# A two-layer graph network on one core: tiles of a half chunk multiplied in reverse, added in forward order, and PSUM banks split by layer

## The chip, the cores and the metric

The kernel runs on one core of one Trainium2 chip. The metric is the device time of one execution in microseconds (us); the time of a kernel is the median of several runs. Beside them there is one profiled execution, taken by the hardware profiler, with its own time and its trace. Engines are called PE (TensorE: matmuls; its weight loads are PEld), DVE (VectorE), ACT (ScalarE), POOL (GpSimd) and SP (SyncE).

## The reference

Two layers of a relational graph convolution over 50,000 nodes with 128 features each, 850,000 edges and 16 relations, then a residual and a layer norm. The weight matrix of each relation is a mix of 8 basis matrices.

```python
def _rgcn_layer(h, src, dst, rel, basis, w_comp, loop_w, bias):
    W = jnp.einsum('rb,bio->rio', w_comp, basis)
    seg = dst * N_REL + rel
    agg = jax.ops.segment_sum(h[src], seg, num_segments=N_ENT * N_REL)
    agg = agg.reshape(N_ENT, N_REL, -1)
    msg = jnp.einsum('nri,rio->no', agg, W)
    return relu(msg + h @ loop_w + bias)

h = _rgcn_layer(x, src, dst, rel, basis1, w_comp1, loop_w1, bias1)
h = _rgcn_layer(h, src, dst, rel, basis2, w_comp2, loop_w2, bias2)
x = _layernorm(x + h, axis=-1, eps=1e-5)
```

The edges come sorted by dst. 50,000 of them are self loops, one for each node, which the kernel handles without a gather; the other 800,000 are gathered, 800,000 / 128 = 6,250 tiles a layer.

## The kernel before

**Tiling.** The features are kept transposed: 128 features on the partitions. A tile is 128 edges in a row (sorted by dst, so that they end in at most WN = 12 neighbouring nodes). Ten tiles (K) are a chunk, five (PER) a half chunk; there are 625 chunks (C) in a layer and 12,500 tiles in all. The layer loop is at L917, the loop over chunks at L1000 and below.

**What is done for a tile.**

- *Gather* (L254, called at L1006). POOL issues an indirect DMA that fetches the 128 source rows. It does so for chunk c+2 while chunk c is multiplied, and a chunk's ten tiles go into one of four buffers g (GATHERS), so tile i lies where tile i-40 lay. Each DMA reports on one of eight semaphores in turn, called lanes below.
- *hot_of* (L923, L930). DVE builds, for a whole chunk, a 128 x 960 matrix `hot`: for each edge its eight basis weights, placed in the column of its node.
- *Multiply* (L1018). PE multiplies g by hot (128x128 by 128x96, float32; the trace shows two weight loads and two matmuls for it) into a piece of a PSUM bank. Five tiles share a bank.
- *Add* (L950). DVE adds the 128 x 96 product to `ring`, an SBUF array with sums for 3 x 512 nodes, at a place read from a register; the registers are loaded at L944, for 20 tiles at a time. An add isn't issued at once: it is put in the list `behind` with a due time of BEHIND = 12 tiles later, and `added_up_to` issues what is due.

**The work of a group** of 512 nodes (98 a layer, about one in 64 tiles) is planned in `Group.planned` with due times counted in tiles: in layer 1 `load`, `turn` (PE transposes, L726) and `combine` (L743); in both `widen` (a broadcast of 1 MB by DMA), `lay` (ACT copies the node features into a bank, L770), `own` (DVE writes the self-loop part into ring from it, L775), `copy` (ACT takes the finished sums out of ring, L792), eight `base` matmuls (L798), `loop` (L803), `relu` (L810), `back` (PE transposes, L822) and `store` (L830 in layer 1). `Weights` makes the per-edge weights for four chunks: in layer 1 `multiply` (L668) and `keep` (L682), in layer 2 a load of what layer 1 stored.

**The order.** PE, POOL, DVE and ACT run their instructions in the order in which the program issues them; what is inserted between are the waits on semaphores. One instruction can carry some of its waits; what is more becomes a wait instruction of its own ahead of it on that engine.

**Banks.** Six PSUM banks named `pa` are handed out by `Turns`: a new one at each half chunk (L1016), and for turn, combine, lay, back and multiply, all from one row in the order of the calls. When `take` hands out a bank again, it first issues the work that must still read it: for a half chunk `Once(added_up_to, ...)`, the adds up to the half's last tile. Six takes later a bank comes round again, which is six halves or fewer, as other work took banks in between.

Of the kernel before, what the change touches and what calls it, by code (L numbers as in the profile page):

```python
# [40 lines left out]
F32 = mybir.dt.float32  # L41
# [7 lines left out]
PSUM = bass.MemoryType.PSUM  # L49
DRAM = bass.MemoryType.DRAM  # L50

P = 128
# [3 lines left out]
K = P // WN  # L56
# [9 lines left out]
PER = 5  # L66
Q = AT // 2
BANK = 512
# [8 lines left out]
BEHIND = 12  # L77
AFTER = 18
AT_ONCE = 4
WIDE = 1  # L80
PARTS_OF = ((0, 3), (3, 5))
# [8 lines left out]
def tile_rgcn_resnorm(  # L90
# [129 lines left out]

    ps_a = ctx.enter_context(tc.tile_pool(name="ps_a", bufs=6, space=PSUM))
    ps_f = ctx.enter_context(tc.tile_pool(name="ps_f", bufs=1, space=PSUM))
# [6 lines left out]
    class Turns:  # L229
        def __init__(self, pool, name, count):  # L230
            self.pool, self.name, self.count, self.held = pool, name, count, []

        def take(self, read=None):

            if len(self.held) == self.count:
                first = self.held.pop(0)
                if first is not None:
                    first()
            self.held.append(read)
            return self.pool.tile([P, BANK], F32, name=self.name)  # L240

# [8 lines left out]

    banks = Turns(ps_a, "pa", 6)

# [5 lines left out]
    def turned(h, m, sb):  # L258

        tp = ps_a.tile([P, BANK], F32, name="pa")  # L260
        nc.tensor.transpose(tp[:, :m], h, ident[:m, :m])
        hT = sb.tile([P, P], F32, name="hT")
        nc.scalar.copy(hT[:, :m], tp[:, :m])
        return hT[:, :m]
# [342 lines left out]
    def chunked():  # L607
        with (
# [20 lines left out]
            class Weights:  # L629
# [32 lines left out]
                def multiply(self):  # L662
                    m = self.m
                    self.po = [banks.take(self.keep) for _ in PARTS_OF]
                    for po, (j0, j1) in zip(self.po, PARTS_OF):
                        of = po[:, : 2 * AT * (j1 - j0) * NB].rearrange("e (n t w) -> e n t w", n=2, t=AT)
                        for j in range(j0, j1):
                            nc.tensor.matmul(  # L668
                                of[:, :, :, (j - j0) * NB : (j - j0 + 1) * NB],
                                self.is_rel[:m, j * P : (j + 1) * P],  # L670
                                each[:m],
                                start=True,
                                stop=True,
                            )
# [17 lines left out]
            class Group:  # L692
# [29 lines left out]
                def turn(self):  # L722
                    m = self.m
                    self.po = banks.take(self.keep)
                    for j in range(J):
                        nc.tensor.transpose(self.po[:, j * P : j * P + m], self.h[:m, j, :], ident[:m, :m])  # L726
# [14 lines left out]
                def combine(self):  # L741
                    self.comb = banks.take(self.combined)
# [25 lines left out]
                def lay(self, b):  # L768
                    self.laid[b] = banks.take(self.owns[b])
                    nc.scalar.copy(self.laid[b][:, : self.cnt], self.hT[:, : self.cnt])  # L770
# [46 lines left out]
                def back(self):  # L817
                    m = self.m
                    self.po = banks.take(self.kept)
                    by_place = self.oT[:, : self.cnt].rearrange("o (p j) -> o j p", j=J)  # L820
# [96 lines left out]
            for n, of in enumerate((x, H1)):  # L917

                def hot_of(c):
# [16 lines left out]
                    hots[c] = hot  # L936

                def add(c, k, pa):

                    i = c * K + k  # L940
                    if i % (2 * K) == 0:
                        left = min(2, C - c) * K
# [54 lines left out]
                for c in range(C):  # L997
# [15 lines left out]
                    hot = hots.pop(c)  # L1013
                    for k in range(K):
                        if k % PER == 0:
                            pa = banks.take(Once(added_up_to, c * K + k + PER - 1))  # L1016
                        if k < ks(c):
# [6 lines left out]
                            )  # L1024
                            behind.append((c * K + k + BEHIND, (c, k, pa)))
                        added_up_to(c * K + k - BEHIND)
                        if c or k == K - 1:
                            go_on(c * K + k)
                    if n == 0 and c == 3:
# [5 lines left out]
                while events or behind:  # L1035
                    added_up_to(now - BEHIND)
                    go_on(now)
                    now += 1
                banks.held = [None] * len(banks.held)
            ordered.close()  # L1040

    def summed():
        L1 = dram.tile([N, D], F32, name="L1")
        L2 = dram.tile([N, D], F32, name="L2")
        with tc.tile_pool(name="io", bufs=2) as io, tc.tile_pool(name="sbf", bufs=2) as sb:
# [73 lines left out]
            def added(h, n, L):  # L1119


                def block(r0, p):
# [13 lines left out]
                    for e in range(ROW):  # L1136
# [4 lines left out]
                        for b in range(NB):  # L1141
                            if b % (BANK // D) == 0:
                                mb = ps_a.tile([P, BANK], F32, name="pa")
                                nc.tensor.matmul(
# [13 lines left out]
                        at = tf[:p, e : e + 1]  # L1158
                        tp = ps_a.tile([P, BANK], F32, name="pa")
                        nc.tensor.transpose(tp[:p, :p], at.to_broadcast([p, p]), ident[:p, :p])  # L1160
# [82 lines left out]
```

## Time and profile before

| | us |
|---|---|
| median of 3 runs | 18,209.43 |
| lowest and highest | 18,202.78, 18,209.78 |
| the profiled execution | 18,065.77 |
| its span, first to last instruction | 18,063.9 |
| mean granted clock of PE | 0.602 of full speed |

In the profile, a group of instructions is a line of the kernel, an engine and an operation, "out<-in" by names, and then the count, the busy time and the mean duration of one in ns, and behind the second bar the idle time of the engine just before these instructions with the releaser that ended most of it. "issue" means that the engine waited for nothing that the profile shows; "remote" is a releaser that it can't name. The chain that ended last is followed back from the last instruction, with shares of the span. A gather moves 128 rows of 512 bytes; all DMA together moved 1,527 MB, 85 GB/s in the mean, and the 16 DMA engines were busy for about 30% of the span, 18.0% with the gathers' queue.

The first gather of layer 1 starts at 58 us, the last of layer 2 ends at 18,023 us. Layer 2 cannot gather before layer 1's last store to H has landed; its first gather starts at 9,110 us.

### The profile page before, as it was taken

The numbers are of one execution on the slowest core, as the hardware profiler recorded it, in microseconds if no ns is written. First come the engines' busy times: TensorE is split into PE (matmuls) and PEld (weight loads), VectorE is DVE, ScalarE is ACT, GpSimd is POOL, SyncE is SP. The second block draws the span as 40 slices with busy tenths as digits, with TensorE's granted clock in tenths as the row PEclk, the third lists the DMA queues.
The fourth block names the chain that finished last, engine by engine and source line by source line (L and its number), as shares of the span: only waits on it lengthen the run. The fifth ranks groups of instructions, "written<-read, shape, count | busy, mean of one in ns | idle before, by whom it ended". The sixth has DMA issues, their size and how long they took to land.

```text
span 18063.9 us, 132710 instructions
## 1 busy us (share of the span) xinstructions
PE 8315.7 (46%) x31484; PEld 6301.1 (35%) x31484; DVE 6563.7 (36%) x18253; ACT 1621.0 (9%) x2256; POOL 11861.6 (66%) x12540
## 2 busy tenths in 40 slices
PE   3444444444444444444444444444444444444444
PEld 2333333333333333333333333333333333333333
DVE  5444444443333333333333333333333333333333
ACT  0110011110100000010000000000000000000000
POOL 6666666666666666666666666666666666666665
PEclk7666666666666666666655555555555555555556
DMA  3333333333323322232322222222222222222222
GB/s 100 94 95 92 92 95 95 94 88 89 85 84 85 85 85 82 85 88 83 84 78 81 81 82 79 81 81 81 81 80 80 81 81 81 81 81 81 81 81 67
DMA packets 793018, 1527.32 MB, mean 85 GB/s; under 512 B 229924, under 2 KB 296342, under 8 KB 792230
## 3 DMA queue, kind: packets, MB, share of 16 engines
q0 software_dynamic: 403552, 826.82, 18.0%
q1 hardware_dynamic: 386934, 691.33, 11.6%
q8 instruction: 259, 4.24, 0.1%
q14 instruction: 529, 4.33, 0.1%
q10 hardware_dynamic: 1744, 0.60, 0.0%
HBM read 1390.97 MB, written 126.86 MB: 84 GB/s over the span
## 4 chain that ended last, share of the span: by engine, by line
issue 37%; PE 28%; another core or an unknown queue 16%; POOL 8%; DVE 5%; DMA 3%; ACT 1%; DVEq 1%; POOLq 0%; ACTq 0%; SPq 0%
PE pa L1018 18%; POOL g L254 8%; PE pn L798 8%; DVE ring L950 2%; DMA g<-H,src 2%; DVE ring L775 1%; PE pa L668 1%; PE pn L803 1%; DMA g<-in_x_dram,src 1%; ACT own L792 0%; PE pa L822 0%; DVE fixed L330 0%; DVEq L944 0%; DVE word L333 0%
## 5 line engine op out<-in xcount | busy, mean ns | idle before, releaser
L1018 PE MATMUL pa<-hot,g 128*128 128x96 f32 x25000 | 5704.8, 361 | 7613.1 <-issue 5607.3
L1018 PEld LDWEIGHTS pa<-hot,g 128*128 128x128 f32 x25000 | 5201.3, 276 | 9323.7 <-issue 7321.4
L254 POOL DMA_INDIRECT g<-in_x_dram,src x6250 | 5929.4, 949 | 3046.5 <-issue 1432.7
L254 POOL DMA_INDIRECT g<-H,src x6250 | 5895.2, 943 | 3045.9 <-issue 1428.8
L950 DVE TENSOR_TENSOR ring<-pa,ring 128x96 f32 x12500 | 3212.4, 257 | 10941.4 <-PE pa L1018 5215.2
L798 PE MATMUL pn<-own,basis 128*128 128x512 f32 x3104 | 2237.5, 799 | 508.1 <-issue 486.0
L930 DVE TENSOR_TENSOR hot<-pm,fixed 128x960 f32<-128x960 f32 x1250 | 1443.0, 1154 | 78.9 <-remote 19.2
L792 ACT COPY own<-ring 128x4096 f32<-128x4096 f32 x194 | 699.6, 3606 | 3172.0 <-DVE ring L950 2131.9
L775 DVE TENSOR_TENSOR ring<-wide,pa 128x2048 f32<-128x2048 f32 x392 | 893.7, 2280 | 84.1 <-issue 28.8
L798 PEld LDWEIGHTS pn<-own,basis 128*128 128x128 f32 x3104 | 656.1, 250 | 701.3 <-issue 696.3
L770 ACT COPY pa<-hT 128x512 f32<-128x512 f32 x392 | 230.8, 589 | 3035.4 <-DVE ring L950 1349.5
L726 PE MATMUL pa<-ident,rows 128*128 128x128 f32 x392 | 107.7, 420 | 829.6 <-ACT t L830 452.2
L810 ACT ACTIVATE oT<-pn,bias_of 128x512 f32<-128x512 f32 x196 | 134.3, 685 | 3928.0 <-PE pa L1018 2237.0
L668 PE MATMUL pa<-each,is_rel 128*128 128x128 f32 x1570 | 348.4, 377 | 291.8 <-issue 151.4
L668 PEld LDWEIGHTS pa<-each,is_rel 128*128 128x128 f32 x1570 | 300.5, 276 | 324.0 <-issue 226.2
L726 PEld LDWEIGHTS pa<-ident,rows 128*128 128x128 f32 x392 | 74.6, 223 | 845.1 <-ACT t L830 457.0
L923 DVE TENSOR_TENSOR fixed<-fixed,key 128x120 f32<-128x120 f32 x1250 | 350.4, 280 | 0.1
L822 PE MATMUL pa<-ident,oT 128*128 128x128 f32 (+1 forms) x784 | 218.6, 406 | 201.4 <-issue 133.9
L803 PE MATMUL pn<-hT,loop 128*128 128x512 f32 x392 | 263.1, 740 | 50.1 <-issue 49.9
L682 ACT COPY pm<-pa 128x192 f32<-128x192 f32 x628 | 141.0, 304 | 1063.8 <-remote 903.3
L822 PEld LDWEIGHTS pa<-ident,oT 128*128 128x128 f32 (+1 forms) x784 | 146.7, 219 | 230.2 <-issue 206.0
L597 ACT ACTIVATE sd<-mv,eps 128x4 f32<-128x4 f32 x98 | 29.1, 297 | 1929.9 <-DVE st L594 969.3
(129 smaller groups left out, 1655.8 us busy)
## 6 DMA issues: line engine op xcount, KB each, us to landing
wide<-CW SPq DMA_DIRECT2D x388, 1024.0 KB
g<-in_x_dram,src POOLq DMA_INDIRECT x6250
g<-H,src POOLq DMA_INDIRECT x6250
rows<-in_x_dram SPq DMA_DIRECT2D x194, 256.0 KB
PM<-pm SPq DMA_DIRECT2D x157, 160.0 KB
pm<-PM SPq DMA_DIRECT2D x157, 160.0 KB
H1T<-oT SPq DMA_DIRECT2D x97, 256.0 KB
H<-t SPq DMA_DIRECT2D x97, 256.0 KB
```

The source lines that it names most:

```text
L254: return nc.gpsimd.indirect_dma_start(out=to, out_offset=None, in_=of, in_offset=bass.IndirectOffsetOnAxis(ap=idx, axis=0))
L668: nc.tensor.matmul(of[:, :, :, (j - j0) * NB : (j - j0 + 1) * NB], self.is_rel[:m, j * P : (j + 1) * P], each[:m], start=True, stop=True,)
L770: nc.scalar.copy(self.laid[b][:, : self.cnt], self.hT[:, : self.cnt])
L775: nc.vector.tensor_tensor(ring[:, b : b + AT_ONCE, self.at : self.at + cnt], self.wide.pop(b)[:, :, :cnt], self.laid.pop(b)[:, None, :cnt] ...
L792: nc.scalar.copy(self.sums, ring[:, :, at : at + cnt])
L798: nc.tensor.matmul(self.pn[:, : self.cnt], BASIS[:, b, :], self.sums[:, b, :], start=b == 0, stop=False)
L803: nc.tensor.matmul(self.pn[:, : self.cnt], LOOP, self.hT[:, : self.cnt], start=False, stop=True)
L822: nc.tensor.transpose(self.po[:m, j * D : (j + 1) * D], by_place[:, j, :], ident)
L923: nc.vector.tensor_tensor(own[:, : ks(c)], grid[:, None, :].to_broadcast([P, ks(c), WN]), key[:, c * K : c * K + ks(c), None].to_broadcast ...
L930: nc.vector.tensor_tensor(hot[:, : ks(c)], pm[:, c % BATCH * K : c % BATCH * K + ks(c), :, None].to_broadcast([P, ks(c), NB, WN]), own[:, ...
L950: nc.vector.tensor_tensor(into, pa[:, k % PER * NB * WN : (k % PER + 1) * NB * WN].rearrange("d (b w) -> d b w", w=WN), into, op=OP.add,)
L1018: nc.tensor.matmul(pa[:, k % PER * NB * WN : (k % PER + 1) * NB * WN], g[:, k, :], hot[:, k].rearrange("e b w -> e (b w)"), start=True, st ...
```

## The change

The change has five parts that belong together.

- Each half chunk's tiles are multiplied last one first: k = 4, 3, 2, 1, 0 and 9, 8, 7, 6, 5. The last chunk of a layer keeps the old order.
- The adds of a half are issued in forward order, k = 0 to 4, the reverse of PE's: each new one is put in front of the half's others in `behind`, and all five carry the due time of the half's end plus BEHIND, where each tile had its own.
- The six banks are six fixed tiles with a counter for each set of banks that is asked for, in place of a pool that turns by itself. `SECTIONS` gives the tiles of layer 1 all six banks, those of layer 2 banks 0 to 3; `OTHERS` gives the other work of layer 1 all six, that of layer 2 (lay, back) banks 4 and 5. `multiply` and `combine` exist in layer 1 only and take its entry. In layer 1 all callers share one counter over six banks, as before.
- The registers with the places are loaded when an add of a new pair of chunks comes, whichever tile that is (`pair`), where it was the pair's first tile.
- At a layer's end the counters are cleared.

```diff
+SECTIONS = (
+    ((6, True, True),),
+    ((4, True, True),),
+)
+OTHERS = (None, (4, 5))
...
     class Turns:
-        def __init__(self, pool, name, count):
-            self.pool, self.name, self.count, self.held = pool, name, count, []
-
-        def take(self, read=None):
-
-            if len(self.held) == self.count:
-                first = self.held.pop(0)
-                if first is not None:
-                    first()
-            self.held.append(read)
-            return self.pool.tile([P, BANK], F32, name=self.name)
+        def __init__(self, tiles):
+            self.tiles, self.held, self.turn = tiles, [None] * len(tiles), {}
+
+        def take(self, read=None, among=None):
+
+            among = tuple(among or range(len(self.tiles)))
+            at = among[self.turn.get(among, 0) % len(among)]
+            self.turn[among] = self.turn.get(among, 0) + 1
+            if self.held[at] is not None:
+                self.held[at]()
+            self.held[at] = read
+            return self.tiles[at]
...
-    banks = Turns(ps_a, "pa", 6)
+    banks = Turns([ps_a.tile([P, BANK], F32, name=f"pa{i}") for i in range(6)])
...
-                    self.po = banks.take(self.keep)
+                    self.po = banks.take(self.keep, OTHERS[self.n])
...
-                    self.laid[b] = banks.take(self.owns[b])
+                    self.laid[b] = banks.take(self.owns[b], OTHERS[self.n])
...
-                    self.po = banks.take(self.kept)
+                    self.po = banks.take(self.kept, OTHERS[self.n])
...
+                pair = [None]
+
                 def add(c, k, pa):
 
                     i = c * K + k
-                    if i % (2 * K) == 0:
+                    if (n, i // (2 * K)) != pair[0]:
+                        pair[0] = n, i // (2 * K)
                         left = min(2, C - c) * K
                         offs = batches[c // BATCH].offs
                         nc.vector.load(at_reg[:left], offs[0:1, c % BATCH * K : c % BATCH * K + left])
...
-                    for k in range(K):
-                        if k % PER == 0:
-                            pa = banks.take(Once(added_up_to, c * K + k + PER - 1))
+                    for at in range(K):
+                        part = SECTIONS[n][c * len(SECTIONS[n]) // C]
+                        k = at // PER * PER + (PER - 1 - at % PER if part[1] and c + 1 < C else at % PER)
+                        if at % PER == 0:
+                            pa = banks.take(
+                                Once(added_up_to, c * K + at + PER - 1), range(part[0])
+                            )
                         if k < ks(c):
                             nc.tensor.matmul(
                                 pa[:, k % PER * NB * WN : (k % PER + 1) * NB * WN],
...
-                            behind.append((c * K + k + BEHIND, (c, k, pa)))
-                        added_up_to(c * K + k - BEHIND)
-                        if c or k == K - 1:
-                            go_on(c * K + k)
+                            if part[2] and c + 1 < C:
+                                behind.insert(len(behind) - at % PER, (c * K + at // PER * PER + PER - 1 + BEHIND, (c, k, pa)))
+                            else:
+                                behind.append((c * K + at + BEHIND, (c, k, pa)))
+                        added_up_to(c * K + at - BEHIND)
+                        if c or at == K - 1:
+                            go_on(c * K + at)
...
                 banks.held = [None] * len(banks.held)
+                banks.turn.clear()
```

More of the change, by code (lines that the diff above doesn't have):

```diff
@@ L219, in weighed @@
             nc.vector.tensor_copy(split[:, n], mine)
-    ps_a = ctx.enter_context(tc.tile_pool(name="ps_a", bufs=6, space=PSUM))
+    ps_a = ctx.enter_context(tc.tile_pool(name="ps_a", bufs=1, space=PSUM))
     ps_f = ctx.enter_context(tc.tile_pool(name="ps_f", bufs=1, space=PSUM))
@@ L258, in turned @@
     def turned(h, m, sb):
-        tp = ps_a.tile([P, BANK], F32, name="pa")
+        tp = banks.take()
         nc.tensor.transpose(tp[:, :m], h, ident[:m, :m])
@@ L663, in multiply @@
                     m = self.m
-                    self.po = [banks.take(self.keep) for _ in PARTS_OF]
+                    self.po = [banks.take(self.keep, OTHERS[0]) for _ in PARTS_OF]
                     for po, (j0, j1) in zip(self.po, PARTS_OF):
@@ L741, in combine @@
                 def combine(self):
-                    self.comb = banks.take(self.combined)
+                    self.comb = banks.take(self.combined, OTHERS[0])
                     nc.tensor.matmul(
@@ L1142, in block @@
                             if b % (BANK // D) == 0:
-                                mb = ps_a.tile([P, BANK], F32, name="pa")
+                                mb = banks.take()
                                 nc.tensor.matmul(
@@ L1158, in block @@
                         at = tf[:p, e : e + 1]
-                        tp = ps_a.tile([P, BANK], F32, name="pa")
+                        tp = banks.take()
                         nc.tensor.transpose(tp[:p, :p], at.to_broadcast([p, p]), ident[:p, :p])
```

## The prediction

> **What bounds the kernel now.** I read the page from the top: busy shares, the chain that ended last, the costliest groups, then the waits.
>
> ```profile
> span 18063.9 us, 132710 instructions
> PE 8315.7 (46%) x31484; PEld 6301.1 (35%) x31484; DVE 6563.7 (36%) x18253; ACT 1621.0 (9%) x2256; POOL 11861.6 (66%) x12540
> ...
> issue 37%; PE 28%; another core or an unknown queue 16%; POOL 8%; DVE 5%; DMA 3%; ACT 1%; DVEq 1%; POOLq 0%; ACTq 0%; SPq 0%
> ...
> L1018 PE MATMUL pa<-hot,g 128*128 128x96 f32 x25000 | 5704.8, 361 | 7613.1 <-issue 5607.3
> L1018 PEld LDWEIGHTS pa<-hot,g 128*128 128x128 f32 x25000 | 5201.3, 276 | 9323.7 <-issue 7321.4
> L254 POOL DMA_INDIRECT g<-in_x_dram,src x6250 | 5929.4, 949 | 3046.5 <-issue 1432.7
> L254 POOL DMA_INDIRECT g<-H,src x6250 | 5895.2, 943 | 3045.9 <-issue 1428.8
> L950 DVE TENSOR_TENSOR ring<-pa,ring 128x96 f32 x12500 | 3212.4, 257 | 10941.4 <-PE pa L1018 5215.2
> ```
>
> No engine is full; POOL, with 66%, has most to do, and does one thing: it issues 12,500 gathers, one for each tile of 128 edges. How fast it could go is read from stretches in which it waits for nobody. The timeline of POOL alone, with its start, length and idle time before:
>
> ```profile
> 66.05 0.94 POOL L254 DMA_INDIRECT g<-in_x_dram,src  x1 [0.30 <-issue]
> 67.30 0.94 POOL L254 DMA_INDIRECT g<-in_x_dram,src  x1 [0.30 <-issue]
> ...
> 6010.32 0.94 POOL L254 DMA_INDIRECT g<-in_x_dram,src  x1 [0.30 <-PE pa L1018]
> 6011.56 0.94 POOL L254 DMA_INDIRECT g<-in_x_dram,src  x1 [0.30 <-issue]
> ...
> 9110.49 0.94 POOL L254 DMA_INDIRECT g<-H,src  x1 [39.26 <-DMA H<-t]
> ```
>
> A gather starts every 1.25 us (66.05, 67.30; 6010.32, 6011.56): 0.945 busy and 0.30 idle. Twelve thousand five hundred of those are 15,612 us (1.249 each). POOL's idle time in front of gathers is 3046.5 + 3045.9 = 6,092 us; 12,500 times 0.30 is 3,750 of it, the one stop between the layers 39, and the other 2,303 us are stalls. So the span is POOL's pace plus 2.3 ms of stalls plus some 100 us at the ends: what the change does to the time is what it does to these stalls, unless it touches the pace.
>
> Whom does POOL wait for, and whom does that one wait for? The waits over the whole span (engine, line, releaser: us in total, times, longest):
>
> ```profile
> PEld pa L1018 <- issue: 7321.4, 7708, 29.7
> PE pa L1018 <- issue: 5607.3, 4629, 29.0
> DVE ring L950 <- PE pa L1018: 5215.2, 1059, 22.6
> ...
> POOL g L254 <- issue: 2861.5, 9120, 3.6
> ...
> POOL g L254 <- remote: 1603.5, 1256, 8.9
> ...
> POOL g L254 <- PE pa L1018: 1295.0, 1639, 8.3
> ```
>
> POOL's stalls stand under PE (1,295) and "remote" (1,604, a releaser the trace can't name): a gather refills the buffer which PE read 40 tiles before, and has no other consumer to wait for. PE in turn waits for nobody in most of its idle time: 5,607 of 7,613 us before matmuls is "issue". What this looks like, in both layers:
>
> ```profile
> 14011.21 0.29 PEld L1018 LDWEIGHTS pa<-hot,g 128*128 128x128 f32 x1 [1.82 <-issue]
> 14011.92 0.32 PE L1018 MATMUL pa<-hot,g 128*128 128x96 f32 x1 [1.80 <-issue]
> ...
> 14012.61 0.29 PEld L1018 LDWEIGHTS pa<-hot,g 128*128 128x128 f32 x1 [1.11 <-issue]
> 14013.31 0.32 PE L1018 MATMUL pa<-hot,g 128*128 128x96 f32 x1 [1.07 <-issue]
> ...
> 14014.26 0.94 POOL L254 DMA_INDIRECT g<-H,src  x1 [1.39 <-remote]
> ...
> 6004.21 4.16 PE L1018 MATMUL pa<-hot,g 128*128 128x96 f32 x18 [0.78 <-issue]
> ```
>
> At 14,011 us PE takes 0.70 us for each instruction (11.21, 11.92, 12.61, 13.31), 2.8 us for a tile's two weight loads and two matmuls, against POOL's 1.25; at 6,004 us eighteen matmuls, nine tiles, take 4.16. The kernel lives on the mean of the two. I call the first the slow gait. Its cause is not in the trace. This is the unknown on which everything hangs.
>
> **The change, part by part.** Instruction counts of the work stay; order, waits and banks change. I counted waits and semaphore updates in the two built programs.
>
> 1. POOL. Gathers that need a wait instruction of their own ahead of them fall from 12,494 to 2,541: with the last tile of a half multiplied first and the first last, only k=0 and k=5 of a chunk wait for PE, for the whole half of four chunks before. Gain to the pace: from 0 to 0.30 us a gather. The gathers of 66 us are of the first chunks, which have no wait for PE in the program; those of 6,010 us have one each; both show 0.30. I take 0. Loss: a gather k=0 now needs PE tile i-36 done where it needed i-40. Four tiles are 4 x 1.249 = 5.0 us less cushion, of 50.0. With PE as the late one, a tenth less cushion costs from nothing (a queue that is always full) to a tenth of the stalls, 230 us. I take 0 here, because the cushion moves a stall forward and lengthens it only where PE catches up in between, and keep 230 for the range.
>
> 2. PE. Its waits on gathers do not fall: each tile still waits for its own of eight DMA lanes, in 12,500 places. Four in five are met beforehand, since the last to land comes first. That order makes PE wait up to four gathers, 5.0 us, longer at a half's start where it has caught up with the gathers. How often that is:
>
> ```profile
> PEld pa L1018 <- DMA g<-H,src: 185.5, 153, 3.2
> ...
> PEld pa L1018 <- DMA g<-in_x_dram,src: 86.8, 82, 3.8
> ```
>
> In 235 of 25,000 weight loads, so at most 235 x 5.0 = 1,175 us of PE's time if each became a half's start; but PE is the late engine of the two, and a PE that has caught up stalls nobody. I take 0. What does fall on PE: separate wait instructions 3,219 to 2,623, its waits for itself (matmul after matmul in the same bank) 1,929 to none, and its semaphore updates 15,256 to 11,487, by 24.7%, since nobody asks for single tiles any more.
>
> What that is worth in the slow gait, no row shows. From one side: nothing, if each instruction is held 0.70 us whatever it waits for or reports; weight loads, which report nothing, stand as long as matmuls there (1.11 and 1.07). From the other: all of the 2,303 us, if the gait comes of waiting and reporting and stops once PE's share of that drops under a limit. I take the share by which reports fall, 24.7% of 2,303 = 569 us, as the stalls sit under PE's completions and not under its multiplying (a 361 ns matmul is short against 2.8 us).
>
> The Trainium skill, "TensorE: Matmul & The Clock Gate", section "The cost: per-tile semaphore tail", gives 26.3 ns for each increment at the end of a matmul, increments being serialized, and holds a single one on the last to be safe. By it 3,769 fewer would be worth 99 us, an estimate from that page, and the sum would be 470 us poorer. The burst above, nine tiles in 4.16 us, shows no such tail; no run here shows the rule at work.
>
> 3. DVE. Adds of a half come due together, 12 tiles after its last; wait instructions fall from 3,214 to 2,415, updates rise from 16,288 to 18,386. It already waited once per half, for PE's last tile. The first tile's add comes four tiles later, 5.0 us, under a DVE that is idle for 64% of the span. Cost 0; if that cover were gone, one add of 257 ns for each update more, 2,098 x 0.257 = 539 us.
>
> 4. Banks. Before, layer 2's tiles and the other work (lay, turn, back) turned over six banks in one row; now tiles have banks 0 to 3 and the rest 4 and 5. A half may begin once the adds of the half four back are done, tile i-16 for its last; before that was i-16, i-21 or i-26. With adds due 12 tiles after the half that leaves 16 - 12 = 4 tiles, 5 us, of slack. Queued behind a waiting PE are all later tiles, the eight basis matmuls of a group, and then the gathers. The waits that exist in that layer, from its own stretch:
>
> ```profile
> L1018 PE MATMUL pa<-hot,g 128*128 128x96 f32 x12485 | 3067.9, 368 | 4103.0 <-issue 3594.9 <-DMA g<-H,src 195.7 <-DVE ring L775 171.3
> L1018 PEld LDWEIGHTS pa<-hot,g 128*128 128x128 f32 x12484 | 2760.6, 284 | 5033.1 <-issue 4554.4 <-DVE ring L775 194.4 <-DMA g<-H,src 183.8
> ```
>
> 171 us of PE's idle time ends with the additions of L775, which read the banks that lay filled and that tiles take next. From one side they vanish with the shared order (gain 171); from the other PE waits one add more at each of 1,250 halves, 1,250 x 0.257 = 321 us. I take 160, half of the second end, for the slack is thinner and the adds of a half now come in one row. In layer 1 six banks stay shared; its tiles stand as before, 0.
>
> Sum: 18,065.77 (this execution's own time) - 569 + 160 = 17,657. The median of the runs shown, 18,209.43, lies 143.66 above the profiled one; that carried over gives **17,800 us**.
>
> **The rivals.** (a) *Everything goes.* If POOL never stalls: 18,065.77 - 2,303 + 143.66 = 15,906 us; half of it 17,058. For it: stalls come in all stretches, of about the same sum in both layers (idle 3,046 each), as if one ratio set them. Against: the 7,321 us of issue idle in front of weight loads have no waiter that the change removes.
>
> (b) *The change does not do what it says.* Five tiles still carry five landing waits on PE, one wait instruction less on POOL leaves its pace at 1.25 us, and the gait is PE's own: 18,209 us. For it: weight loads stand as long as matmuls.
>
> (c) *Slower: layer 2's four banks.* PE runs up against the add of the half four back at each half's start while the gather of k=0 asks for tile i-36. Price: 321 + 230 = 551 us; time 18,761, without the second part 18,530. It decides once DVE is later than four tiles, 5.0 us, behind its due place; its longest wait for PE is 22.6 us, so in the slow gait it is. Against: a DVE that waits for PE (5,215 us) is not what holds PE up, and PE's waits for L775 are only 171 us.
>
> (d) *Slower: the clock.* The granted clock goes with PE's pauses:
>
> ```profile
> 58.00:9082.00 9024.00, 4007.72 (x16761) 3120.27 (x16761) 3427.76 (x9280) 897.27 (x1358) 5945.17 (x6271) 0.62 0.31 89
> ...
> 9120.00:18023.00 8903.00, 4265.60 (x14597) 3155.98 (x14596) 3067.88 (x8772) 702.10 (x861) 5887.86 (x6243) 0.58 0.28 80
> ...
> L1018 PE MATMUL pa<-hot,g 128*128 128x96 f32 x12500 | 2633.9, 354 | 3496.4 <-issue 2012.4 <-ACT pm L682 536.1 <-ACT lrel L754 297.1
> L1018 PEld LDWEIGHTS pa<-hot,g 128*128 128x128 f32 x12500 | 2437.9, 268 | 4276.5 <-issue 2754.5 <-ACT pm L682 558.7 <-ACT lrel L754 315.2
> ```
>
> From layer 1 to 2 the clock falls from 0.62 to 0.58, a matmul grows from 354 to 368 ns and a load from 268 to 284: 30 ns a pair for 0.04. If tiles bunched in fives bring it to 0.50, that is 60 ns more a pair, 25,000 x 0.060 = 1,500 us of PE, of which its 28% of the chain is 420: 18,630 us. The Trainium skill, the same page, section "HAM oscillation — how this bites in real kernels", has this rule: pauses over about 3.4 us between short bursts send the clock to half each time. The trace's mean of 0.602 agrees that the gate is at work; a busy share of 46% says that it costs little more.
>
> **How the numbers follow.** A measurement of this kernel tells 0.2%, 36 us, from no change. Chances: my forecast, with its own range 17,200 (1,000 us gained) to 18,170, 0.44; (a) 0.20; (b) 0.06; (c) 0.22; (d) 0.08. Faster 0.64, same 0.06, slower 0.30. The range goes from 16,600, which leaves some 0.08 of (a) below, to 18,550, which leaves some 0.10 of (c) and (d) above.
>
> **What would show it.** Right: POOL's idle sum in front of gathers falls from 6,092 to about 5,700, with the pace still 1.25 us; PE's "issue" idle before L1018 falls by a fifth or so; layer 2 gains less than layer 1. Wrong, by step: a pace other than 1.25 (1); PE waiting for g's DMA in many more than 235 places (2); the 0.70 us gait in as much of the span as before, with the idle sum unchanged (2, then b holds); PE's waits for L950 in layer 2 above 321 us (4, then c holds); a granted clock near 0.50 (d). What makes all of it wrong is a gait that has to do with neither reports nor waits, but with the order in which tiles, loads and banks are touched.

## The result and the profile after

| | us |
|---|---|
| before, median of 5 runs | 18,202.78 |
| changed, median of 5 runs | 18,112.62 |
| ratio | 0.995, 95% interval 0.9939 to 0.9961 |
| changed, span of the profiled execution | 18,110.7 |

The change made the kernel 0.5% faster, 90 us, where 2.2% was forecast. In the two profiled executions even that is not to be seen: 18,063.9 us before, 18,110.7 after. The one of before lies below all five of its runs (18,189.99 to 18,209.78), the other on the median of its own.

The page of the changed kernel (its L260 is L254 of before, L1031 is L1018, L959 is L950), with the same columns as before:

```profile
span 18110.7 us, 121429 instructions
PE 8135.5 (45%) x31484; PEld 6161.3 (34%) x31484; DVE 6662.5 (37%) x18253; ACT 1612.4 (9%) x2256; POOL 11875.1 (66%) x12540
...
L1031 PE MATMUL pa<-hot,g 128*128 128x96 f32 x25000 | 5483.5, 354 | 7602.5 <-issue 5889.6
L1031 PEld LDWEIGHTS pa<-hot,g 128*128 128x128 f32 x25000 | 5052.5, 271 | 9275.5 <-issue 7326.2
L260 POOL DMA_INDIRECT g<-in_x_dram,src x6250 | 5941.7, 951 | 3066.7 <-issue 1712.0
L260 POOL DMA_INDIRECT g<-H,src x6250 | 5896.3, 943 | 3075.0 <-issue 1678.8
```

POOL's idle time in front of gathers is 3066.7 + 3075.0 = 6,142 us, where it was 6,092. None of the stalls went, and PE's "issue" idle is 5,890 us in front of matmuls where it was 5,607, and 7,326 us in front of weight loads where it was 7,321. (The second is a poor measure of the gait in the new order: e5 below, without the gait, has 6,381 us of it.) What did change is how the stalls come, in the waits of POOL (us in total, times, longest):

```profile
POOL g L260 <- issue: 3390.8, 11105, 1.7
POOL g L260 <- remote: 1179.1, 380, 9.3
POOL g L260 <- PE pa L1031: 1167.2, 343, 12.1
```

Those with a releaser are 723 (380 + 343) of 3.2 us in the mean, 2,346 us together; before they were 2,895 of 1.0 us, 2,899 us together. The rest became "issue", which is nearly all pace: with so many gathers no longer waiting, 11,105 of them show some 0.30 us each. Counted by their start times alone, gathers that start over 0.15 us late fell from 1,898 to 850. POOL's timeline shows the new form:

```profile
14004.96 0.94 POOL L260 DMA_INDIRECT g<-H,src  x1 [0.30 <-issue]
14006.21 0.94 POOL L260 DMA_INDIRECT g<-H,src  x1 [0.30 <-issue]
14011.16 0.94 POOL L260 DMA_INDIRECT g<-H,src  x1 [4.00 <-remote]
14012.41 0.94 POOL L260 DMA_INDIRECT g<-H,src  x1 [0.31 <-issue]
14013.65 0.94 POOL L260 DMA_INDIRECT g<-H,src  x1 [0.30 <-issue]
```

One long stall, and then gather after gather at 1.25 us. The waits were merged, as the change says, and their sum stayed. So something that they do not set decides the sum. The experiments look for it.

PE's own waits changed too. The first two rows are of after, the third of before:

```profile
PE pa L1031 <- issue: 5889.6, 4406, 19.5
PE pa L1031 <- DVE ring L959: 1208.3, 516, 34.1
...
PE pa L1018 <- DVE ring L950: 51.8, 28, 16.1
```

PE's matmuls now wait 1,208 us for DVE's adds, 587 of it in layer 1 and 621 in layer 2, where it was 52. Other waits of theirs went: those for ACT's pm, lrel and hT fell from 946 to 70 us, those for DVE's self-loop part (`own`, L775, now L781) from 307 to 2. The idle time before matmuls as a whole stayed, 7,613 us before and 7,602 after.

One thing limits the reading of both traces: most updates of semaphores are missing from them. The trace of after holds 50,543, that of before 56,008; the same changed kernel holds 258,110 in e5 below. A wait whose release was not recorded can show as "issue", so that word does not prove that nothing was waited for; nor are the times under each releaser whole. The packets of the gathers' queue are complete (403,552 in all three). By them, sixteen data packets to a gather in order of time, a tile's gather had landed 33 us before PE loaded the tile's weights in the kernel before, and 28 us in the changed one, in the median, and 12 us or more for 99 tiles in 100. So it was not the gathers that PE waited for.

### The profile page after: what moved, and what is told of

Its sections match the earlier page's. It is cut to its first block, busy times and chain, and to the rows that moved or that the text cites. A ratio compares the mean times of both kernels' runs of the same rounds, so it can differ in the third digit from the quotient of the medians.

```text
span 18110.7 us, 121429 instructions
## 1 busy us (share of the span) xinstructions
PE 8135.5 (45%) x31484; PEld 6161.3 (34%) x31484; DVE 6662.5 (37%) x18253; ACT 1612.4 (9%) x2256; POOL 11875.1 (66%) x12540
## 3 DMA queue, kind: packets, MB, share of 16 engines
q0 software_dynamic: 403552, 826.82, 15.9%
## 4 chain that ended last, share of the span: by engine, by line
issue 38%; PE 19%; POOL 18%; another core or an unknown queue 12%; DVE 10%; DMA 2%; DVEq 1%; ACT 0%; POOLq 0%; SPq 0%; ACTq 0%
POOL g L260 18%; PE pa L1031 12%; DVE ring L959 5%; PE pn L804 5%; DVE ring L781 1%; DVE hot L936 1%; DMA g<-H,src 1%; DMA g<-in_x_dram,src 1%; PE pn L809 1%; PE pa L674 1%; DVE fixed L336 1%; DVE word L339 0%; DVE fixed L929 0%; DVEq L953 0%
## 5 line engine op out<-in xcount | busy, mean ns | idle before, releaser
L1031 PE MATMUL pa<-hot,g 128*128 128x96 f32 x25000 | 5483.5, 354 | 7602.5 <-issue 5889.6
L1031 PEld LDWEIGHTS pa<-hot,g 128*128 128x128 f32 x25000 | 5052.5, 271 | 9275.5 <-issue 7326.2
L260 POOL DMA_INDIRECT g<-in_x_dram,src x6250 | 5941.7, 951 | 3066.7 <-issue 1712.0
L260 POOL DMA_INDIRECT g<-H,src x6250 | 5896.3, 943 | 3075.0 <-issue 1678.8
L959 DVE TENSOR_TENSOR ring<-pa,ring 128x96 f32 x12500 | 3220.1, 258 | 10695.1 <-remote 5531.4
L781 DVE TENSOR_TENSOR ring<-wide,pa 128x2048 f32<-128x2048 f32 x392 | 892.3, 2276 | 100.6 <-issue 34.6
L339 DVE COPY_PREDICATED word<-fixed,word 128x224 int32<-128x224 int32 (+9 forms) x450 | 178.4, 396 | 51.9 <-DVE fixed L336 18.8
```

The source lines that it names most:

```text
L260: return nc.gpsimd.indirect_dma_start(out=to, out_offset=None, in_=of, in_offset=bass.IndirectOffsetOnAxis(ap=idx, axis=0))
L781: nc.vector.tensor_tensor(ring[:, b : b + AT_ONCE, self.at : self.at + cnt], self.wide.pop(b)[:, :, :cnt], self.laid.pop(b)[:, None, :cnt] ...
L959: nc.vector.tensor_tensor(into, pa[:, k % PER * NB * WN : (k % PER + 1) * NB * WN].rearrange("d (b w) -> d b w", w=WN), into, op=OP.add,)
L1031: nc.tensor.matmul(pa[:, k % PER * NB * WN : (k % PER + 1) * NB * WN], g[:, k, :], hot[:, k].rearrange("e b w -> e (b w)"), start=True, st ...
```

## The experiments

Each set of runs was taken on one chip, with the kernel before beside them. This turned out to matter more than any edit: the kernel before took 18,203 us in the first comparison and 18,272 in one later set (e13, e14), and 15,801 to 15,834 in the seven others. The record numbers the chips: 0 for e13 and e14; 10 (twice), 12, 15 (twice), 3 and 6 for the seven others; none for the first comparison. Whether that was chip 0 is not known, and as chip 0 was met once, neither is whether the slow time belongs to a chip or to a state that it was in. "A chip with the gait" below means a chip as it was in that set.

### The parts of the change, less work for PE, and a shorter cushion

e1 has the banks without the order:

```diff
-    ((6, True, True),),
-    ((4, True, True),),
+    ((6, False, False),),
+    ((4, False, False),),
```

e2 has the order without the split of the banks (the six fixed tiles stay):

```diff
-    ((4, True, True),),
+    ((6, True, True),),
 )
-OTHERS = (None, (4, 5))
+OTHERS = (None, None)
```

e3 leaves out two of five multiplies:

```diff
+                    j = (0, 0, 2, 2, 4)[k % PER]
...
-                        pa[:, k % PER * NB * WN : (k % PER + 1) * NB * WN].rearrange("d (b w) -> d b w", w=WN),
+                        pa[:, j * NB * WN : (j + 1) * NB * WN].rearrange("d (b w) -> d b w", w=WN),
...
-                        if k < ks(c):
+                        if k < ks(c) and k % PER not in (1, 3):
```

e4 has three gather buffers:

```diff
-GATHERS = 4
+GATHERS = 3
```

> The changed kernel with both order flags off: tiles are multiplied and added in the order of before, each due 12 tiles later; only the fixed banks and the split of layer 2 (tiles on banks 0 to 3, the rest on 4 and 5) remain. Theory A (the order gains and the four banks give most of it back): slower than before by 100 to 550 us, so 18300 to 18750. Theory B (PE delivers its tiles at a mean rate that waits and banks do not set, so POOL's stalls keep their sum): within 100 us of before, about 18200, with some 1900 stalls of about 1.2 us as in the kernel before.

> The changed kernel with the order reversed in both layers, but all six banks shared by tiles and the rest in layer 2 as before. Theory A: faster than the changed kernel by 100 to 550 us, 17550 to 18000. Theory B: within 100 us of the changed kernel, 18010 to 18210, with POOL's stalls again few and long (850 of about 2.8 us) and the same sum of about 2350.

> The changed kernel with two of five tiles not multiplied (k=1 and k=3 of a half; their adds read a neighbour's product, so that DVE and POOL do as much as before): 10,000 matmuls and as many weight loads fewer on PE. Theory B with a cost per PE instruction (0.70 us gait for a share of them): POOL's stalls fall by far more than a third, time 15900 to 16900. Theory C (the stalls come of a loop of latencies between PE, DVE, ACT and POOL, not of PE's amount of work): 17600 or more.

> The changed kernel with three gather buffers in place of four, so that a gather of k=0 waits for PE's tile 26 before it and not 36. Theory B: PE's rate is what it is, so the time stays within 200 us of the changed kernel (17910 to 18310), the queue being always full. Theory D (the stalls are what a cushion of 36 to 40 tiles lets through of PE's slow stretches of some 20 us): stalls grow by far over a quarter, time 18700 to 20500.

Measured, beside 15,834.19 us for before on that chip: e1 15,835.46 (ratio 1.0001, 0.9991 to 1.001), e2 15,842.77 (1.0006, 0.9996 to 1.0015), e3 15,847.54 (1.0008, 0.9998 to 1.0018), e4 15,854.35 (1.0013, 1.0002 to 1.0023). No expected time held, of any theory, as all were worked out from 18,200; of theory B only "within 100 us of before" is left. Nothing that is taken from PE or added to its waits moves the time by more than 0.13%. The waits of PE in e1 say why; it waits for gathers, where it stood under "issue":

```profile
PE pa L1031 <- DMA g<-H,src: 2764.5, 3672, 12.5
PE pa L1031 <- DMA g<-in_x_dram,src: 2430.5, 3086, 25.9
```

PE has caught up with POOL, no gather is held up, and the time is POOL's pace: 12,500 gathers of 1.25 us and the ends.

### The changed kernel itself on another chip

> The changed kernel itself, beside the kernel before on one chip. Before measured 18202.78 us where the change was first timed and 15834.19 us on the chip of the last four runs, whose profiles show hardly any 0.70 us gait on PE. Theory E (the stalls come with PE's slow gait, which one chip has and another has not; without it POOL's pace of 1.25 us sets the time): where before takes about 15834 us, the change is within 0.2% of it; where before takes about 18200, it is 0.5% faster again. Theory A (the order saves waiting that is there on any chip): 0.5% or more faster than before where before takes 15834 us too.

Measured: 15,813.26 us, before 15,805.45, ratio 1.0005 (0.9995 to 1.0015). Theory E holds, theory A does not. Rows of this run's page, its waits and a stretch of PE's timeline:

```profile
L1031 PE MATMUL pa<-hot,g 128*128 128x96 f32 x25000 | 5611.6, 388 | 7547.3 <-DMA g<-H,src 3537.3
L1031 PEld LDWEIGHTS pa<-hot,g 128*128 128x128 f32 x25000 | 5195.8, 295 | 9295.8 <-issue 6380.9
L260 POOL DMA_INDIRECT g<-in_x_dram,src x6250 | 5933.0, 949 | 1945.4 <-issue 1679.1
L260 POOL DMA_INDIRECT g<-H,src x6250 | 5899.3, 944 | 1930.2 <-issue 1677.0
...
PE pa L1031 <- DMA g<-H,src: 3537.3, 1050, 14.1
PE pa L1031 <- DMA g<-in_x_dram,src: 3251.7, 941, 24.9
...
14001.95 2.42 PE L1031 MATMUL pa<-hot,g 128*128 128x96 f32 x10 [5.24 <-DMA g<-H,src]
14006.75 2.42 PE L1031 MATMUL pa<-hot,g 128*128 128x96 f32 x10 [2.38 <-DMA g<-H,src]
```

POOL idles 1945.4 + 1930.2 = 3,876 us, of which 3,750 are the pace. PE's 0.70 us steps are gone: of its matmuls and weight loads, 72 start 0.65 to 0.75 us after the one before, where 4,707 do in the trace of before and 4,828 in that of the changed kernel in the first comparison. And here one sees the change at work: PE waits for the last gather of a half and then multiplies five tiles, ten matmuls, in one burst of 2.42 us. Its waits for gathers are 1,991 (1050 + 941), where in the old order of e1 they were 6,758 (3672 + 3086). The order does what the change says, and on a chip where PE is not late that is worth nothing.

e10 was e3's kernel once more, in case the chip was one with the gait:

> The kernel of e3 again (two of five tiles not multiplied), in case the chip is one with the slow gait, which shows in the time of the kernel before. Where before takes some 18200: if the gait costs per PE instruction, stalls fall by a third or more, below 17300; if it is a thing of time and not of work, 17800 to 18200. Where before takes 15800 to 15834: 15790 to 15860 as in e3, and the gait is then absent from this chip too.

It was not: before 15,833.09, e10 15,844.35 us, inside the range for such a chip.

### A PE that is late all the time

The gait can't be switched on. What can be tried anywhere is what a late PE does to the waits: each multiply issued six times, in the kernel before (e6), in the changed one (e7), in the changed one with e2's edit (e8) and with e4's (e9). The last product of the six stands, so that the sums are the same.

```diff
                         if k < ks(c):
+                          for again in range(6):
                             nc.tensor.matmul(
...
+                            if again < 5:
+                                continue
```

> The kernel before, with each tile's multiply issued six times (the last product stands), so that PE, not POOL, is the late engine on a chip without the slow gait: 6 x 0.22 us, the burst's pace, and some 0.2 us of other work a tile are about 1.5 us against POOL's 1.25, 18500 to 21000 us (to 33000 if PE stays at half clock). In both theories stalls of POOL number thousands, on gathers of all k. It is the partner of the next run.

> The changed kernel with each tile's multiply issued six times. Theory E (where PE is late, POOL's stalls add up to PE's time less POOL's, whoever reports how often; the change only gathers them at k=0 and k=5): within 0.5% of the run before this one, with POOL's stalls fewer by half or more and each longer, and the same sum within 10%. Theory A (fewer reports and waits let a late PE run faster): faster than its partner by 2% or more. Theory F (four banks and a cushion of 36 cost a late PE): slower by 1% or more.

> The late-PE form of the changed kernel (each multiply six times) with all six banks shared in layer 2, so that only the order differs from the kernel before. Theory E: within 0.3% of the changed kernel's late-PE form (18844.62) on its chip, its ratio to before 1.190 to 1.196. If the four banks of layer 2 cost a late PE (rival c of the prediction), this one is faster than that by 1% or more, ratio below 1.181.

> The late-PE form of the changed kernel with three gather buffers, a gather of k=0 then waiting for PE's tile 26 before it. Theory E: a queue that is always full needs no length: ratio to before within 0.3% of 1.1926. If a tenth less cushion costs a tenth of the stalls (the other bound of the prediction's first part), a quarter less costs some 700 us: 19550, ratio 1.237.

Measured: e6 18,776.41 us, e7 18,844.62 on the same chip, so 0.4% slower; on another chip e8 18,843.86 and e9 18,843.03 (ratios to before 1.1883, 1.1926, 1.1925, 1.1925, each within 0.002). First e6, then e7, groups and POOL's waits:

```profile
L1019 PEld LDWEIGHTS pa<-hot,g 128*128 128x128 f32 x150000 | 17074.3, 192 | 866.7 <-issue 791.0
...
L254 POOL DMA_INDIRECT g<-in_x_dram,src x6250 | 5932.0, 949 | 3454.6 <-PE pa L1019 3161.1
L254 POOL DMA_INDIRECT g<-H,src x6250 | 5909.5, 946 | 3282.1 <-PE pa L1019 2958.2
...
POOL g L254 <- PE pa L1019: 6119.3, 11056, 9.2
```

```profile
PE 18661.7 (99%) x156484; PEld 17784.9 (94%) x156484; DVE 6716.7 (36%) x18253; ACT 1621.6 (9%) x2256; POOL 11891.8 (63%) x12540
...
L260 POOL DMA_INDIRECT g<-in_x_dram,src x6250 | 5960.5, 954 | 3538.0 <-PE pa L1032 1916.8
L260 POOL DMA_INDIRECT g<-H,src x6250 | 5894.7, 943 | 3298.9 <-PE pa L1032 1644.1
...
POOL g L260 <- PE pa L1032: 3560.9, 2326, 16.8
```

This has the form of the first comparison, with a PE whose lateness is made by the edit: 11,056 waits for PE become 2,326, and POOL's idle sum goes from 6,737 to 6,837 us. With PE busy for 99% of the span, the stalls are PE's time less POOL's; how often PE reports (13,355 semaphore updates by its matmuls in e6, 3,492 in e7), how many banks layer 2 has (e8 against e7) and how long the queue of buffers is (e9) win nothing. Of the 68 us that e7 is slower, 39 are nine waits of PE for DVE's adds, which e8 has too. Theory E holds in all four, A and F do not. In the count, one of E's numbers was missed: the waits for PE are fewer by far over half, but the gathers that came over 0.15 us late are not: 2,253 in e6, 2,561 in e7, since most of e6's many waits are shorter than that.

### A PE that is late in stretches

The gait comes and goes, so the same was done in stretches: 15 times in three chunks of nine, once in the other six.

```diff
+                          for again in range(15 if c % 9 < 3 else 1):
```

> The kernel before with PE late in stretches: in three of nine chunks each multiply is issued 15 times (30 tiles x (15 x 0.22 + 0.2) = 105 us), in six once (60 x 0.4 = 24 us, less than their gathers). POOL can run 40 tiles ahead: 37 + 30 gathers of 1.25 us are 84 us, so it stalls some 21 us in each of 139 stretches of layers 1 and 2: 18500 to 19100. Theory E in its plain form (PE's mean, 1.43 us a tile) gives 17950 to 18200 at least.

> The changed kernel with the same stretches. If the cushion counts where PE is late in stretches longer than it, the 36 tiles that a gather of k=0 or k=5 leaves cost 4 x 1.25 = 5 us in each of 139 stretches: 690 us more than the run before this one, ratio of the two about 1.037. If not, within 0.5% of it, as with an evenly late PE. On the chip of the first comparison the change was 0.5% faster: were its slow stretches of this kind, the cushion would have shown there.

Measured: e11 19,680.62 us, e12 20,780.16 on the same chip, 5.6% slower. e11 came out some 600 us above its range; the stalls were 28 us a stretch where 21 were worked out (idle 7,696 us less 3,750 for the pace and 82 between the layers, by the expectation's 139 stretches; the loops make 140, 70 a layer). e12 was expected 690 us above e11, and is 1,100 above it. First e11, then e12, groups, one of PE's waits and, of e12, three rows of POOL's timeline:

```profile
L254 POOL DMA_INDIRECT g<-in_x_dram,src x6250 | 5928.5, 949 | 3973.7 <-PE pa L1019 2638.7
L254 POOL DMA_INDIRECT g<-H,src x6250 | 5896.2, 943 | 3722.5 <-PE pa L1019 2293.5
...
PE pa L1019 <- DMA g<-H,src: 96.1, 98, 12.4
```

```profile
L260 POOL DMA_INDIRECT g<-in_x_dram,src x6250 | 5938.7, 950 | 4466.1 <-PE pa L1032 2626.8
L260 POOL DMA_INDIRECT g<-H,src x6250 | 5897.3, 944 | 4326.7 <-PE pa L1032 2402.3
...
PE pa L1032 <- DMA g<-H,src: 558.9, 157, 14.3
...
14013.96 0.95 POOL L260 DMA_INDIRECT g<-H,src  x1 [0.30 <-issue]
14025.72 0.94 POOL L260 DMA_INDIRECT g<-H,src  x1 [10.81 <-PE pa L1032]
14026.96 0.94 POOL L260 DMA_INDIRECT g<-H,src  x1 [0.30 <-issue]
```

The idle sums differ by 1,097 us, which is all of the difference in time, 7.8 us a stretch. The timeline shows the form: POOL stands 10.8 us until a whole half is multiplied and then refills five places at 1.25 us. Before, each tile gave its place back by itself. When PE turns fast again it finds fewer gathers done and waits for them, 559 us in layer 2 where e11 waits 96: what POOL lost is no longer regained. To see which part does it, the change was split:

> The changed kernel with late stretches as in e12, but all six banks shared in layer 2: only the order differs from e11. If the order costs (a gather of k=0 or k=5 waits for a whole half on PE, 5 tiles of 3.4 us each in a late stretch, where before each tile freed its own place): as slow as e12, ratio to before 1.30 to 1.33, with POOL's stalls at k=0 and k=5 alone. If the four banks cost (PE waits for adds): near e11, 1.245 to 1.26, in layer 2 above all.

> The partner: the order of before with the four banks of layer 2, late stretches as in e11. If the order costs: ratio to before as in e11, 1.245 within 0.005. If the banks cost: slower than that by 2% or more, all of it in layer 2.

This set met a chip with the gait (before 18,271.86): e13 27,336.15 us (ratio 1.4961, 1.4936 to 1.4986), e14 26,791.17 (1.4654, 1.463 to 1.4678). Neither set of numbers could hold there; the order on six fixed tiles is 2.0% slower than the split banks with the old order. So both were run once more, together with e1's and e2's kernels. e13 and e15 are e12 with e2's edit, e14 and e16 are e12 with e1's:

> The kernel of e13 once more, since that call met a chip with the slow gait (before 18272 us). On a chip without it (before about 15800): if the order costs the 5.6% of e12, ratio to before 1.30 to 1.33; if the four banks cost it, 1.245 to 1.26. With the gait again: 1.49 to 1.50.

> The kernel of e14 once more. On a chip without the slow gait: if the order costs the 5.6% of e12, ratio to before 1.24 to 1.25; if the four banks cost it, 1.28 or more, with all of the loss in layer 2. With the gait again: 1.46 to 1.47.

> The kernel of e1 (four banks in layer 2, old order). On a chip with the slow gait: if the order made the 0.5% of the first comparison, this one is within 0.2% of before, or slower; if the banks made it, 0.3% to 0.7% faster. On a chip without: ratio 1.000 within 0.002, as e1.

> The kernel of e2 (order reversed, six shared banks). On a chip with the slow gait: if the order made the 0.5%, 0.3% to 0.7% faster than before; if the banks made it, within 0.2%. On a chip without: ratio 1.000 within 0.002, as e2.

This time the chip had no gait (before 15,804.43). The order without the split took 20,775.92 us (1.3145, 1.3123 to 1.3167), as e12 did (1.315); the banks with the old order 20,019.13 (1.2666, 1.2645 to 1.2687) against e11's 1.2454. e15 came out as expected of a loss by the order; e16 lies between its two ranges. So splitting the banks adds nothing to the reversed order (e12 against e15), and turning the order round on the same banks costs 3.8% (e12 against e16). The other 1.7% of the 5.6% is there with the old order already. e15 still has the fixed tiles, and no run has the new order on the old pool, so how much of the 1.7% the order would cost by itself is not shown. The 1.7% is no loss of layer 2 alone, as the expectation of e16 had it: its POOL idle, next, is above e11's in both layers, 185 us in layer 1, where tiles have six banks as before and hardly more than the fixed tiles differs, and 151 in layer 2. The last two rows, of e16 and of e11, name what PE waits for instead: DVE's adds. Why the fixed tiles should bring that about was not taken apart.

```profile
L260 POOL DMA_INDIRECT g<-in_x_dram,src x6250 | 5925.5, 948 | 4158.7 <-PE pa L1032 2866.0
L260 POOL DMA_INDIRECT g<-H,src x6250 | 5896.1, 943 | 3873.9 <-PE pa L1032 2532.8
...
PE pa L1032 <- DVE ring L959: 829.4, 362, 8.1
...
PE pa L1019 <- DVE ring L950: 19.3, 18, 4.9
```

e17 and e18 were 15,806.25 and 15,811.11 us, ratios 1.0001 and 1.0004 within 0.001: nothing, as e1 and e2.

The pair e14 and e16 is of use in another way: it is one kernel on a chip with the gait and on one without, 26,791 and 20,019 us. PE's weight loads, e14 first, with two rows of its PE timeline, then e16:

```profile
PEld pa L1032 <- issue: 5242.9, 6616, 12.5
...
14080.50 0.32 PE L1032 MATMUL pa<-hot,g 128*128 128x96 f32 x1 [2.47 <-issue]
14081.91 0.32 PE L1032 MATMUL pa<-hot,g 128*128 128x96 f32 x1 [1.08 <-issue]
```

```profile
PEld pa L1032 <- issue: 831.8, 3199, 12.7
```

The single matmuls 1.4 us apart are back (80.50, 81.91), and the idle time without a releaser is six times as long, with the same instructions and the same waits. Steps of 0.65 to 0.75 us are 3,311 in e14 and 32 in e16. Here too over half of the semaphore updates are missing where the gait is: e14's trace holds 117,286, e16's 257,968.

## Why the prediction was wrong

The time was 18,112.62 us, inside the range, faster as forecast, but 90 us instead of 409. By its own steps:

- *What bounds the kernel* was right for that chip: POOL's pace of 1.25 us and 2.3 ms of stalls behind a PE in its slow gait. The pace is seen in every profile since, and it alone makes the 15,8xx us of the other chips. What the prediction took for a property of the kernel, the gait, comes with the chip or its state: it is absent in seven sets on five chips, and there in two sets, in the kernel before and in the changed one. That PE "waits for nobody" was more than the trace could tell, with most semaphore updates missing; the packets bear it out for the gathers alone.
- *Step 1, POOL.* Right that 9,953 wait instructions fewer leave the pace alone: 1.25 us after the change (12.41, 13.65). The cushion at 0 holds where PE is late evenly (e9). Its other bound, a tenth of the stalls, was too small for long stretches: 1,097 us (e12), of which turning the order round on the same banks makes 761 (e12 against e16), because the price is that of places freed by halves and not of four tiles at POOL's pace.
- *Step 2, PE,* is the step that failed: "I take the share by which reports fall, 24.7% of 2,303 = 569 us". The stalls did not fall at all in the profiled pair (2,303 before; 6,142 - 3,750 - 37 = 2,355 after), and by the medians of the runs they fell by 90 us at most. Nor did the gait: the steps of 0.65 to 0.75 us were 4,707 before and are 4,828 after. With a late PE whose reports fall by the same edit, from 13,355 to 3,492, e7 is not faster than e6 but 0.4% slower. Reports are not what the late PE loses its time on; the end that was named for the other side, "each instruction is held 0.70 us whatever it waits for or reports", is the one that the runs bear out. The 26.3 ns that the Trainium skill gives per increment ("TensorE: Matmul & The Clock Gate", "The cost: per-tile semaphore tail") would be 99 us for 3,769, and 259 us for the 9,863 fewer of e7, both estimates from that page. e6 and e7, whose PE is busy for 99%, show no such gain, so they don't bear it out at this spacing.
- *Step 2 in its small part,* that PE's waits on gathers are met beforehand for four tiles of five, was right: 6,758 waits in e1, 1,991 in e5.
- *Steps 3 and 4.* Where PE is late evenly, DVE's later adds cost 39 us, and of the 160 us for four banks e8 against e7 shows none. In the first comparison, though, the sign that the prediction named for step 4 did come: in layer 2 PE's waits for the adds are 621 us, above its 321, and layer 1, which it put at 0, has 587. As PE's idle time stayed what it was, these waits took the place of others. What they would cost alone on that chip no run shows.
- *The rivals.* (b) was nearest in its time, and in its main reason, that the gait is PE's own. (a) gave 15,906 us for a kernel without stalls; that is nearly what the other chips measure, but the chip does it and not the change. (c), which ends on the slow side, saw its sign (the waits for adds) but not its time; in stretches a loss came, 3.8% by the order and 1.7% with waits for adds in both layers, not by the four banks of layer 2 that it named. (d) did not come: the granted clock was 0.602 before and is 0.608 after.
- *The offset.* The sum was made against an execution of 18,065.77 us and 143.66 were added. The runs of the changed kernel lie within 9 us of each other and of its profiled execution, so that offset belonged to one execution of before.

What stays open: which part of the change makes the 0.5% in the first comparison, and whether waits for adds took part of a larger gain there. e17 and e18 would have told, and met a chip without the gait. And what the gait is: neither its 0.70 us nor what sets it off shows in a releaser.

## What to carry to other kernels

When an engine waits for a late one, merging its waits changes their number and need not change their sum: 1,898 late gathers became 850 here, and 2.3 ms of stalls stayed 2.3 ms. Ask first why the late engine is late, and if its idle time is "issue" in even steps, run the same kernel on another chip before explaining it. Count the semaphore updates in the trace as well: where most are missing, "issue" says little. And a wait that stands for five tiles also gives five places back at once: that cost 0.4% at most where the late engine was late evenly, nothing measurable where it was not late, and 3.8% where it was late in stretches longer than the buffers.

## What was not expected of the hardware

One kernel took 15,801 to 15,834 us on five chips and 18,203 to 18,272 in two sets, a difference of 15%. The difference is on PE: steps of 0.70 us from instruction to instruction with no waiter named, while gathers land and POOL paces as on the others. A backlog before PE does not bring the steps about by itself: e6, with PE late from end to end on a chip without the gait, has 791 us of "issue" idle in front of 150,000 weight loads, and 192 ns for a load where the kernel before took 276. The gait and the missing semaphore updates come together in all four profiles that show it (before, after, e13 and e14: 50,543 to 117,286 updates) and in none of the others (249,572 or more). Whether what slows PE also loses the records, or the recording slows PE, no run here shows. With PE busy for 99% the granted clock was 0.996 to 0.998; it is 0.59 to 0.619 in the kernels whose PE is busy for 41 to 61% of the time.
